# Seven products of quarters for three merged feed-forward weights, and one quad of tokens turned by VectorE

## The chip, the core and the metric

The kernel runs on one core of a Trainium2 chip. A core has several engines that each execute their own queue of instructions in order: TensorE (PE, matrix products; its weight loads are listed apart as PEld), VectorE (DVE), ScalarE (ACT), GpSimd (POOL) and SyncE (SP), which here only issues DMA transfers. They wait for each other by semaphores. Work lies in SBUF (128 partitions); PE writes into PSUM, of which the kernel uses two sides of four banks of 128x512 fp32 each. The metric is the device time of one execution in microseconds (us); lower is better. Everything is in fp32.

## The reference

The input x is 2 x 1024 tokens of 256. Four layers follow each other, each added to x:

```python
x = x + _L0_xattn_ref(_layernorm(x), ctx_1024, Wq, Wk, Wv, Wo, bo)    # attention in 4 windows, 8 heads of 64
x = x + _L0_ffn_ref(_layernorm(x), W1, b1, W2, b2)
x = x + _L1_xattn_ref(_layernorm(x), ctx_1024, ctx_1024, Wq, Wk, Wv, Wo)  # sigmoid scores, 16 heads of 16
x = x + _L1_ffn_ref(_layernorm(x), gamma_x, gamma_slot, slot_embeds, w1, w2)  # soft mixture of experts, 1024 slots

def _L0_ffn_ref(x, W1, b1, W2, b2):        # 8 groups of 256 tokens, each with weights of its own
    xg = x.reshape(8, 256, 256)
    h1 = jnp.einsum('gmh,goh->gmo', xg, W1) + b1[:, None, :]    # 1024 inner features
    h2 = jnp.einsum('gmo,gho->gmh', h1, W2) + b2[:, None, :]
    return h2.reshape(orig_shape)
```

The second layer has no non-linear step between its two products.

## The kernel before

**Tiling.** The 2048 tokens are four quads of 512 (`xq[0]` to `xq[3]`), each 4 tiles of 128 tokens. Quad q holds the tokens of the feed-forward groups 2q and 2q+1. The whole of x stays in SBUF.

**The feed-forward of layer 0.** Since it is linear, the two weights of a group g are first merged into one 256x256 matrix M_g = W1^T W2, with the bias row worked in. `product(g)` (L875) does it: 16 matmuls of 128x128 by 128x256 (L882; 8 chunks of the inner 1024 by 2 halves of the rows) sum into one PSUM bank `pmt`, a copy brings it to SBUF as `mt_g`, and POOL adds the bias b2 on one row (L891). Then `prepare(g+1)` subtracts, in place, the first column of the next group's W1 from the others (ACT at L865 and L869). The weights of a group lie in a tile `wg` (both factors and the first column apart), of which three exist, so that later groups load while earlier ones are used.

`norm_ff(q)` (L899) makes the normed tokens of a quad: `layernorm` (L824) calls `normed` (L814), which takes the moments on DVE, a power -1/2 on POOL and then subtracts and scales on DVE into `hn`; POOL sets the first column to 1; and `transposed` (L128) turns the 512 tokens with eight PE transposes into two PSUM banks `pt_f`, copied to `hT_f`. `feed_forward(q)` (L903) then takes, for both of the quad's groups, four matmuls with `hT_f` as the stationary operand and `mt_g` as the moving one, into `po`, and DVE adds `po` to x (L917).

**Turning tokens without PE.** Two other ways are in the kernel. `turned` (L149) lets DVE turn every 32x32 square in place of its tile, four instructions per quad (L137), into a tile `tr`; sixteen transfers of 32 KB, issued by SP (L158), then bring the squares to their places in the turned quad. `turned_by_square` (L163) takes the same four DVE instructions, then one transfer to DRAM (L170, `d_a`) and four back (L172). `turned` is used in layer 1's mixture of experts (`tr_m` to `xhT`), `turned_by_square` for the queries of layer 1 (`tr_a` to `hTa`) and the slots (`tr_se`). The tiles `hn`, `hT` and `tr` each come from the pool `lnp`, which has two buffers for each of these names: a third `tr` takes the buffer of the first and waits until the transfers out of that one have ended.

**The order of the work.** Around the change the source reads (L1120 to L1142, then L1266 to L1349): attention of layer 0 for quad after quad, between it the products 1 to 4, then `product(5)`, `feed_forward(1)`, `product(6)`, `norm_ff(2)`, `feed_forward(2)`, `slot_norms`, `norm_queries(0)`, `product(7)`, `norm_ff(3)`, `norm_queries(1)`, `norm_queries(2)`, the sums `pvs` (L1281), `queries(0)` (`pq`, L1240), and then the loop over quads of layer 1's attention. There, for q = 0: scores `psg` of the first half (L1308), their tanh on ACT (L1317), `feed_forward(3)`, the outputs `poT` (L1340), scores of the second half, `queries(1)`, and so on. This order is not the order of execution: a scheduler of the framework puts each engine's instructions into a queue at build time, by its own estimates of when each could run, and the engines then execute these queues strictly in order. Only a few instructions are pinned to the order of the source (`keep_in_program_order`, used with `late`), and the later stages have an order written by hand. So a change in one place can move other instructions in the queues, of DVE and of SP's transfers too. SP's queue issues the transfers of both turnings; a transfer that must wait for its data holds up those behind it.

**The names in the changed stretch** (60 to 120 us of the profile): `wg` weights, `pmt` and `mt` merged weights, `e` the softmax terms of layer 0's attention, `hn_f`, `pt_f`, `hT_f` the normed, turned tokens of the feed-forward, `po` its outputs, `tr_a`, `d_a`, `hTa` the queries' turned tokens, `pq` and `psg` the queries and scores of layer 1.

Of the kernel before, what the change touches and what calls it, by code (L numbers as in the profile page):

```python
# [9 lines left out]
FP = mybir.dt.float32  # L10
AF = mybir.ActivationFunctionType
ALU = mybir.AluOpType
# [3 lines left out]
P = 128  # L16
B = 2
S = 1024
D = 256
DC = D // P  # L20
NK = 64
QT = 4
# [12 lines left out]
OC = FF // P  # L35
# [10 lines left out]
SQ = 32  # L46
R4 = P // SQ
# [5 lines left out]
def tile_kernel(  # L53
# [19 lines left out]
    nc = tc.nc  # L73
# [9 lines left out]
    def bank(name, side=0):  # L83
        return ps[side].tile([P, 512], FP, tag="bank", name=name)
# [43 lines left out]
    def transposed(src, dst, name, side=0, out=nc.any.tensor_copy):  # L128

        for c in range(DC):  # L130
            pt = bank(f"pt_{name}_{c}", side)
            for t in range(QT):
                nc.tensor.transpose(pt[:, ts(t, P)], src[:, t, ts(c, P)], ident)
            out(dst[:, c, :], pt)
# [7 lines left out]
    def squares(src, tr, late=False):  # L142

        for t in range(QT):
            turn = square(src[:, t, 0:D], tr, t)
            if late:
                tc.keep_in_program_order(turn)

    def turned(src, dst, tr):  # L149

        squares(src, tr)
        to = dst.rearrange("p c (t i n) -> p (c t) i n", t=QT, i=R4)
        for i in range(R4):
            for r in range(R4):
                nc.sync.dma_start(  # L158
                    out=to[ts(r, SQ), :, i, :],
                    in_=tr[ts(i, SQ), r].rearrange("p c t n -> p (c t) n"),  # L160
                )
# [434 lines left out]
    def tt(dst, x, y, op):  # L596
        nc.vector.tensor_tensor(dst, x, y, op)  # L597
# [201 lines left out]
    with (  # L799
# [24 lines left out]
        def layernorm(xt, name, side=0, out=nc.any.tensor_copy):  # L824

            hn = normed(xt, name, 1)
            nc.gpsimd.memset(hn[:, :, 0:1], 1.0)
            hT = lnp.tile([P, DC, QN], FP, tag="hT", name=f"hT_{name}")
            transposed(hn, hT, name, side, out)
            return hT  # L830

# [2 lines left out]
        ffc = wide.enter_context(tc.tile_pool(name="ffc", bufs=1))  # L834
        weights = {}
# [20 lines left out]
        def prepare(g):  # L856
            if g not in weights:
                load_group(g)
            w1g, _, first = weights[g]
            less = ffc.tile([P, OC], FP, name=f"less_{g}")  # L860
            for part, scalar in enumerate((g > 0, g > 0)):
                ocs = range(part * OC // 2, (part + 1) * OC // 2)
                some = slice(ocs.start, ocs.stop)
                if scalar:
                    nc.scalar.activation(less[:, some], first[:, some, 0], AF.Copy, scale=-1.0)  # L865
                for oc in ocs:
                    w = w1g[:, oc, 1:]
                    if scalar:
                        last_prepared[g] = nc.scalar.activation(  # L869
                        w, w, AF.Identity, bias=less[:, oc : oc + 1]  # L870
                    )
                    else:
                        nc.vector.tensor_scalar(w, w, first[:, oc, :], None, ALU.subtract)  # L873

        def product(g):  # L875
            if g == 0:
                prepare(0)
            w1g, w2g, _ = weights[g]
            pm = bank(f"pmt_{g}", 1)
            for oc in range(OC):  # L880
                for hc in range(DC):
                    nc.tensor.matmul(  # L882
                        pm[:, ts(hc, D)],
                        lhsT=w1g[:, oc, ts(hc, P)],
                        rhs=w2g[:, oc, :],
                        start=(oc == 0 and hc == 0),
                        stop=(oc == OC - 1 and hc == DC - 1),
                    )
            mt = ffc.tile([P, DC, D], FP, name=f"mt_{g}")
            nc.any.tensor_copy(mt, pm.rearrange("p (c n) -> p c n", c=DC))  # L890
            nc.gpsimd.tensor_tensor(mt[0:1, 0, :], mt[0:1, 0, :], b2r[:, g, :], ALU.add)  # L891
            mts.append(mt)
            if g + 1 < NG:
                prepare(g + 1)


        hTfs = {}

        def norm_ff(q, side=0):  # L899
            out = nc.any.tensor_copy if q < QB else nc.scalar.copy  # L900
            hTfs[q] = layernorm(xq[q], f"f0_{q}", side, out)

        def feed_forward(q, side=0):  # L903
            for i in range(QN // GN):
                g = q * (QN // GN) + i
                xg = xq[q][:, ts(i, 2), :]
                po = bank(f"po_{g}", side)
                for t in range(2):
                    for dc in range(DC):
                        nc.tensor.matmul(  # L910
                            po[:, ts(t, D)],
                            lhsT=hTfs[q][:, dc, ds(i * GN + t * P, P)],
                            rhs=mts[g][:, dc, :],
                            start=(dc == 0),
                            stop=(dc == DC - 1),
                        )
                nc.vector.tensor_tensor(  # L917
                    xg, xg, po.rearrange("p (t d) -> p t d", t=2), ALU.add
                )
# [7 lines left out]
        with tc.tile_pool(name="p0", bufs=1) as p0, tc.tile_pool(name="a0", bufs=2) as a0:  # L927
# [25 lines left out]
            load_quad(3)  # L953

            product(0)


# [22 lines left out]
            for c in range(C0):  # L980
                for dc in range(DC):
                    nc.tensor.matmul(
                        pk[:, ts(c, P)],
                        lhsT=wk0s[:, dc, ts(c, P)],
                        rhs=hcT[:, dc].rearrange("p b j -> p (b j)"),
                        start=(dc == 0),
                        stop=(dc == DC - 1),
# [5 lines left out]
            for c in range(C0):  # L993
                for dc in range(DC):
                    nc.tensor.matmul(
                        pv[:, ts(c, P)],
                        lhsT=wv0s[:, dc, ts(c, P)],
                        rhs=hcT[:, dc].rearrange("p b j -> p (b j)"),
                        start=(dc == 0),
                        stop=(dc == DC - 1),  # L1000
# [9 lines left out]
            for dc in range(DC):  # L1010
                pws = [bank(f"pwk_{dc}_{e}") for e in range(2)]
                for c in range(C0):
                    for e in range(2):
# [3 lines left out]
                            lhsT=wq0s[r, c, ts(dc, P)],  # L1017
                            rhs=kT[r, c, :],
                            start=True,
                            stop=True,  # L1020
# [8 lines left out]
            for g in range(NBW // 2):  # L1029
                pw = bank(f"pvw_{g}")  # L1030
                for i in range(2):
                    for c in range(C0):
                        nc.tensor.matmul(
                            pw[ds(32 * c, 32), ts(i, D)],
                            lhsT=vblk[:, c, 2 * g + i].rearrange("p e j -> p (e j)"),
                            rhs=wo0s[:, c, :],
                            start=True,
                            stop=True,
# [61 lines left out]
            def attend(q):  # L1100
                if q not in atTs:
                    turn_weights(q)
                atT = atTs[q]
                for i in range(2):
                    po = bank(f"po0_{q}_{i}")
                    for k in range(2):
                        t = 2 * i + k
                        nc.tensor.matmul(  # L1108
                            po[:, ts(k, D)],
                            lhsT=atT[:, ts(t, P)],  # L1110
                            rhs=vw[:, (q * QT + t) // 2, :],
                            start=True,
                            stop=True,
                        )
                    xi = xq[q][:, ts(i, 2), :]
                    nc.vector.tensor_tensor(
                        xi, xi, po.rearrange("p (t d) -> p t d", t=2), ALU.add
                    )
# [16 lines left out]
            load_layer1()  # L1135
            norm_ff(1)
            attend(3)
        product(5)
        feed_forward(1)
        product(6)  # L1140
        norm_ff(2)
        feed_forward(2)  # L1142

        with (
            tc.tile_pool(name="a1c", bufs=1, side="right") as a1c,
# [35 lines left out]
            for c in range(C1):  # L1181
                for dc in range(DC):
                    nc.tensor.matmul(
                        pk[:, ts(c, P)],
                        lhsT=wk1s[:, dc, ts(c, P)],
                        rhs=ctxd[:, dc],
                        start=(dc == 0),
                        stop=(dc == DC - 1),
# [13 lines left out]
            for dc in range(DC):  # L1202
                nc.tensor.matmul(
                    pv[:, 0:D],
                    lhsT=ctxd[:, dc].rearrange("p b s -> p (b s)"),
                    rhs=wv1s[:, dc, :],
                    start=(dc == 0),
                    stop=(dc == DC - 1),
# [5 lines left out]
            for b in range(B):  # L1214
                for e in range(2):
                    to = vblk1[e * NK : (e + 1) * NK, b, :, e, :]
# [63 lines left out]
            for c in range(C1):  # L1280
                nc.tensor.matmul(  # L1281
                    pvs[:, ts(c, B)],
                    lhsT=vals[:, ts(c, NPR)].rearrange("p r e d -> p (r e d)"),
                    rhs=in_batch,
                    start=True,
                    stop=True,
# [7 lines left out]
            for q in range(NQ):  # L1294
                b = q * QN // S
                oTs[q] = a1.tile([P, C1, QN], FP, tag="oT", name=f"oT_{q}")
                for c in range(C1):
# [8 lines left out]
                    for j in range(NPR):  # L1306
# [3 lines left out]
                            lhsT=kblk[r, c, b].rearrange("p e s -> p (e s)"),  # L1310
                            rhs=qTs[q][r, c, :],
                            start=True,
                            stop=True,
# [25 lines left out]
                    for j in range(NPR):  # L1339
                        nc.tensor.matmul(  # L1340
                            po[ds(32 * j, 32), :],
                            lhsT=vblk1[:, b, NPR * c + j].rearrange("p e d -> p (e d)"),
                            rhs=sg[:, j, :],
                            start=True,
                            stop=True,
# [153 lines left out]
```

## Time and profile before

| | us |
|---|---|
| median of 3 runs | 423.4 (423.31 to 423.4) |
| profiled execution, device time | 423.25 |
| its span, first to last instruction | 421.5 |
| PE busy / DVE / ACT / POOL | 415.9 / 315.6 / 131.1 / 74.1 |
| product of one group on the chain (16 matmuls, L882) | 6.91 |
| all `pmt` matmuls (L882, 256 records) | 58.3 |
| eight transposes of quad 3's tokens on the chain (L133) | 0.87 |
| transfer of 32 KB by L158 (`xhT`), issue to landing, median | 2.0 |
| transfers back from DRAM by L172 (`hTa`), median | 3.1 |

The profile gives start and length of each instruction of one execution, with the engine and the line of the source, and for idle time the event that ended it. The device time contains 1.75 us that lie outside the span of the instructions. Busy shares say how full an engine is; the chain of waits, followed back from the last instruction, says which work set the end. Waiting on an engine that isn't on this chain costs nothing by itself. Durations of short DVE instructions overlap slightly: one takes 0.68 us from start to end at 128x512, and the next can start 0.60 us after it did; the distance from start to start is called the pitch here.

### The profile page before, as it was taken

The numbers are of one execution on the slowest core, as the hardware profiler recorded it, in microseconds if no ns is written. First come the engines' busy times: TensorE is split into PE (matmuls) and PEld (weight loads), VectorE is DVE, ScalarE is ACT, GpSimd is POOL, SyncE is SP. The second block draws the span as 40 slices with busy tenths as digits, with TensorE's granted clock in tenths as the row PEclk, the third lists the DMA queues.
The fourth block names the chain that finished last, engine by engine and source line by source line (L and its number), as shares of the span: only waits on it lengthen the run. The fifth ranks groups of instructions, "written<-read, shape, count | busy, mean of one in ns | idle before, by whom it ended". The sixth has DMA issues, their size and how long they took to land.

```text
span 421.5 us, 6298 instructions
## 1 busy us (share of the span) xinstructions
PE 415.9 (99%) x2270; PEld 310.3 (74%) x2270; DVE 315.6 (75%) x711; ACT 131.1 (31%) x266; POOL 74.1 (18%) x86
## 2 busy tenths in 40 slices
PE   8999999999999999999999999999999999999996
PEld 7889988888444454444488644899998864499996
DVE  2677777745578669978769889977985589776956
ACT  1145938513544522344641654300000004420000
POOL 2113233211101220104948900000000000000000
PEclk9999999999999999999999999999999999999999
DMA  6999983413633332120052764450022576520003
GB/s 256 416 415 425 402 340 134 168 47 112 149 102 105 46 47 31 29 43 2 0 213 101 129 97 74 65 89 2 0 84 49 121 120 98 89 44 2 2 2 100
DMA packets 99425, 50.03 MB, mean 119 GB/s; under 512 B 87873, under 2 KB 94401, under 8 KB 97857
## 3 DMA queue, kind: packets, MB, share of 16 engines
q1 hardware_dynamic: 99394, 49.63, 42.2%
q8 instruction: 18, 0.29, 0.3%
q14 instruction: 13, 0.11, 0.1%
HBM read 32.74 MB, written 6.30 MB: 93 GB/s over the span
## 4 chain that ended last, share of the span: by engine, by line
PE 86%; DVE 7%; SPq 2%; DMA 2%; issue 1%; POOL 1%; ACT 0%; DVEq 0%
PE psl L409 13%; PE pmt L882 13%; PE pc L586 12%; PE pp L586 12%; PE pmh L511 10%; PE pl L256 7%; PE pq L1240 3%; PE po L910 3%; SPq L158 2%; PE psc L1058 2%; PE pf L1254 2%; PE po L1108 2%; PE psg L1308 2%; PE poT L1340 1%; DMA wg<-in_wff_dram 1%
## 5 line engine op out<-in xcount | busy, mean ns | idle before, releaser
L882 PE MATMUL pmt<-wg 128*128 128x256 f32 x256 | 58.3, 384 | 0.3 <-DVE wg L873 0.3
L409 PE MATMUL psl<-xh,lg 128*128 128x258 f32 x256 | 56.8, 381 | 0.0
L256 PE MATMUL pl<-seT,xhT 128*128 128x512 f32 x128 | 56.1, 594 | 0.2 <-DVE rmax L275 0.2
L882 PEld LDWEIGHTS pmt<-wg 128*128 128x128 f32 x256 | 48.8, 193 | 7.5 <-DVE wg L873 0.7
L409 PEld LDWEIGHTS psl<-xh,lg 128*128 128x128 f32 x256 | 48.2, 190 | 7.4 <-issue 0.5
L256 PEld LDWEIGHTS pl<-seT,xhT 128*128 128x128 f32 x128 | 24.1, 190 | 29.2 <-issue 25.7
L395 POOL TENSOR_TENSOR lg<-lg,mb 128x1024 f32<-128x1024 f32 x13 | 33.2, 2594 | 26.9 <-ACT mb L203 25.3
L279 ACT ACTIVATE ec<-lg,nm 128x1024 f32<-128x1024 f32 x16 | 18.4, 1149 | 39.7 <-DVE nm L264 37.7
L586 PEld LDWEIGHTS pp<-ms,mh 128*128 128x128 f32 x256 | 29.4, 192 | 1.6 <-issue 1.0
L586 PE MATMUL pp<-ms,mh 128*128 128x128 f32 x256 | 30.2, 276 | 0.3
L521 ACT ACTIVATE mh<-mh 128x512 f32<-128x512 f32 x32 | 19.2, 627 | 21.1 <-DVE mh L557 19.6
L511 PE MATMUL pmh<-slT,ms 128*128 128x512 f32 x48 | 24.2, 592 | 0.0
L869 ACT ACTIVATE wg<-wg,less 128x255 f32<-128x255 f32 x56 | 23.4, 495 | 0.1
L1317 ACT ACTIVATE sg<-psg 128x512 f32<-128x512 f32 x32 | 16.5, 603 | 18.2 <-PE psg L1308 18.2
L586 PE MATMUL pp<-m_sums,mh 128*128 128x128 f32 x192 | 22.1, 275 | 0.0
L586 PE MATMUL pc<-pr,ec 128*128 128x128 f32 x192 | 22.1, 275 | 0.0
L586 PEld LDWEIGHTS pc<-pr,ec 128*128 128x128 f32 x192 | 21.8, 192 | 0.0
L586 PEld LDWEIGHTS pp<-m_sums,mh 128*128 128x128 f32 x192 | 21.8, 192 | 0.0
L398 ACT ACTIVATE lg<-lg 128x1024 f32<-128x1024 f32 x16 | 16.1, 1045 | 18.3 <-POOL lg L395 18.3
L545 ACT COPY mh<-pmh 128x512 f32<-128x512 f32 x8 | 4.6, 569 | 50.2 <-PE pmh L511 50.2
L308 DVE STREAM_TRANSPOSE tr<-ec 128x512 f32<-128x512 f32 x32 | 19.7, 674 | 0.0
L597 DVE TENSOR_TENSOR mh<-mh,mh 128x1024 f32<-128x1024 f32 x16 | 18.5, 1218 | 0.5 <-PE pp L586 0.5
(193 smaller groups left out, 669.8 us busy)
## 6 DMA issues: line engine op xcount, KB each, us to landing
wg<-in_wff_dram SPq DMA_DIRECT2D x5, 2052.0 KB, 10.1
ec<-tr SPq DMA_DIRECT2D x128, 64.0 KB, 2.3
wg<-in_wff_dram SPq DMA_DIRECT2D x4, 1026.0 KB, 12.9
xT<-in_xT_dram SPq DMA_DIRECT2D x4, 512.0 KB, 13.9
x<-in_x_dram SPq DMA_DIRECT2D x4, 512.0 KB, 16.1
d_a<-tr_a SPq DMA_DIRECT2D x4, 512.0 KB, 2.6
hTa<-d_a SPq DMA_DIRECT2D x16, 128.0 KB, 3.1
xhT<-tr_m SPq DMA_DIRECT2D x64, 32.0 KB, 2.0
```

The lines of the kernel that those rows point to most:

```text
L256: nc.tensor.matmul(pl, lhsT=xhTs[q][:, dc, ts(t, P)], rhs=in_order(seT[:, n], dc), start=(dc == 0), stop=(dc == DC - 1),)
L279: nc.scalar.activation(ecs[q][:, :, t, :], lg.rearrange("p (h n) -> p h n", h=2), AF.Exp, bias=nm[:, 1:2], scale=-1.0, accum_out=zcs[b][:, ...
L308: ins = nc.vector.transpose(tr[:, :, :, t, :].rearrange("p r c n -> p c r n"), half[:, t, :].rearrange("p (c r n) -> p c r n", c=EC // 2, ...
L395: engine.tensor_tensor(lgs[b][s], lgs[b][s], mbs[b], ALU.add)
L409: nc.tensor.matmul(pz[:, 0:XW], lhsT=lgs[b][s][:, ts(c, P)], rhs=xhs[b * QB + s // QT][:, s % QT, :], start=(s == 0), stop=(s == ST - 1),)
L511: nc.tensor.matmul(to, lhsT=lefts[i][:, ts(j, P)], rhs=in_order(slTs[b][0], i) if i < 2 else rights[b][i], start=True, stop=True,)
L521: nc.scalar.activation(h, h, AF.Gelu)
L586: nc.tensor.matmul(to, lhsT=left(k, m), rhs=right[:, k, :], start=(k == 0), stop=(k == QT - 1),)
L597: nc.vector.tensor_tensor(dst, x, y, op)
L869: last_prepared[g] = nc.scalar.activation(w, w, AF.Identity, bias=less[:, oc : oc + 1])
L882: nc.tensor.matmul(pm[:, ts(hc, D)], lhsT=w1g[:, oc, ts(hc, P)], rhs=w2g[:, oc, :], start=(oc == 0 and hc == 0), stop=(oc == OC - 1 and hc ...
L1317: nc.scalar.activation(sg[:, j, :], psgs[j], AF.Tanh, scale=0.5 * DH1**-0.5)
```

## The change

For groups 5, 6 and 7 (`FEWER`) the merged weight is made from quarters. Both factors are cut in two along the inner 1024 features (the sum) and in two along the 256 columns, and M_g, cut into four 128x128 blocks, is made from seven products of quarters instead of eight (Winograd's form of Strassen's method). `sum_quarters(g)` makes the sums and differences of quarters, eight DVE instructions of 128x512 each (two of them in place in the weights, six in a new tile `qs`), and is called right after `prepare(g)`. `product_of_quarters(g)` takes 7 x 4 matmuls of 128x128 by 128x128 into two PSUM banks; an ACT copy and seven DVE additions of 128x128, which read PSUM, make the four blocks of `mt_g`. The bias add on POOL stays. The tile `qs` of group 6 lies in a pool `qp` that is opened before `product(5)` and closed after `feed_forward(2)`, those of 5 and 7 share one in `ffc`.

For the last quad of the feed-forward (`f0_3`) `layernorm` calls `turned` in place of `transposed`: four DVE square transposes into a `tr` tile of `lnp` and sixteen transfers on SP instead of eight PE transposes and two copies.

```diff
@@ -826,6 +826,11 @@
             hn = normed(xt, name, 1)
             nc.gpsimd.memset(hn[:, :, 0:1], 1.0)
             hT = lnp.tile([P, DC, QN], FP, tag="hT", name=f"hT_{name}")
+            if name in ('f0_3',):
+
+                tr = lnp.tile([P, R4, DC, QT, SQ], FP, tag="tr", name=f"tr_{name}")
+                turned(hn, hT, tr)
+                return hT
             transposed(hn, hT, name, side, out)
             return hT
 
@@ -872,26 +877,88 @@
                     else:
                         nc.vector.tensor_scalar(w, w, first[:, oc, :], None, ALU.subtract)
 
+        FEWER = (5, 6, 7)
+        HO = OC // 2
+        quarter_sums, sums_in = {}, [ffc]
+
+        def quarters(w):
+
+            return [[w[:, ts(k, HO), ts(i, P)] for i in range(2)] for k in range(2)]
+
+        def sum_quarters(g):
+            w1g, w2g, _ = weights[g]
+            qs = sums_in[-1 if g == 6 else 0].tile([P, 6, HO, P], FP, tag="qs", name=f"qs_{g}")
+            s1, s2, s4, t1, t2, t4 = (qs[:, i] for i in range(6))
+            (b11, b12), (b21, b22) = quarters(w2g)
+            tt = nc.vector.tensor_tensor
+            tt(t1, b12, b11, ALU.subtract)
+            tt(t2, b22, t1, ALU.subtract)
+            tt(b12, b22, b12, ALU.subtract)
+            tt(t4, b21, t2, ALU.subtract)
+            (a11, a21), (a12, a22) = quarters(w1g)
+            tt(s1, a21, a22, ALU.add)
+            tt(s2, s1, a11, ALU.subtract)
+            tt(a21, a11, a21, ALU.subtract)
+            tt(s4, a12, s2, ALU.subtract)
+            quarter_sums[g] = [
+                (a11, b11), (a12, b21), (s2, t2), (a21, b12), (s1, t1), (s4, b22), (a22, t4)
+            ]
+
+        def product_of_quarters(g):
+
+            pms = [bank(f"pmt_{g}_{i}", 1) for i in range(2)]
+            p1, p2, p6, p7, p5, p3, p4 = (
+                pms[i // 4][:, ts(i % 4, P)] for i in range(7)
+            )
+            for to, (left, right) in zip((p1, p2, p6, p7, p5, p3, p4), quarter_sums[g]):
+                for k in range(HO):
+                    nc.tensor.matmul(
+                        to,
+                        lhsT=left[:, k, :],
+                        rhs=right[:, k, :],
+                        start=(k == 0),
+                        stop=(k == HO - 1),
+                    )
+            mt = ffc.tile([P, DC, D], FP, name=f"mt_{g}")
+            u = ffc.tile([P, 3, P], FP, tag="u", name=f"u_{g}")
+            (c11, c12), (c21, c22) = [[mt[:, c, ts(i, P)] for i in range(2)] for c in range(2)]
+            u1, u2, u3 = (u[:, i] for i in range(3))
+            tt = nc.vector.tensor_tensor
+            nc.scalar.copy(u1, p1)
+            tt(u2, p6, u1, ALU.add)
+            tt(c11, p2, u1, ALU.add)
+            tt(u3, p7, u2, ALU.add)
+            tt(c22, p5, u3, ALU.add)
+            tt(u2, p5, u2, ALU.add)
+            tt(c12, p3, u2, ALU.add)
+            tt(c21, p4, u3, ALU.add)
+            return mt
+
         def product(g):
             if g == 0:
                 prepare(0)
             w1g, w2g, _ = weights[g]
-            pm = bank(f"pmt_{g}", 1)
-            for oc in range(OC):
-                for hc in range(DC):
-                    nc.tensor.matmul(
-                        pm[:, ts(hc, D)],
-                        lhsT=w1g[:, oc, ts(hc, P)],
-                        rhs=w2g[:, oc, :],
-                        start=(oc == 0 and hc == 0),
-                        stop=(oc == OC - 1 and hc == DC - 1),
-                    )
-            mt = ffc.tile([P, DC, D], FP, name=f"mt_{g}")
-            nc.any.tensor_copy(mt, pm.rearrange("p (c n) -> p c n", c=DC))
+            if g in FEWER:
+                mt = product_of_quarters(g)
+            else:
+                pm = bank(f"pmt_{g}", 1)
+                for oc in range(OC):
+                    for hc in range(DC):
+                        nc.tensor.matmul(
+                            pm[:, ts(hc, D)],
+                            lhsT=w1g[:, oc, ts(hc, P)],
+                            rhs=w2g[:, oc, :],
+                            start=(oc == 0 and hc == 0),
+                            stop=(oc == OC - 1 and hc == DC - 1),
+                        )
+                mt = ffc.tile([P, DC, D], FP, name=f"mt_{g}")
+                nc.any.tensor_copy(mt, pm.rearrange("p (c n) -> p c n", c=DC))
             nc.gpsimd.tensor_tensor(mt[0:1, 0, :], mt[0:1, 0, :], b2r[:, g, :], ALU.add)
             mts.append(mt)
             if g + 1 < NG:
                 prepare(g + 1)
+                if g + 1 in FEWER:
+                    sum_quarters(g + 1)
 
 
         hTfs = {}
@@ -1135,11 +1202,14 @@
             load_layer1()
             norm_ff(1)
             attend(3)
+        qp = ExitStack()
+        sums_in.append(qp.enter_context(tc.tile_pool(name="qp", bufs=1)))
         product(5)
         feed_forward(1)
         product(6)
         norm_ff(2)
         feed_forward(2)
+        qp.close()
 
         with (
             tc.tile_pool(name="a1c", bufs=1, side="right") as a1c,
```

## The prediction

> **What bounds the kernel now.** I read the page first: the span, the busy shares and slices, and the shares of the chain of waits.
>
> ```profile
> span 421.5 us, 6298 instructions
> PE 415.9 (99%) x2270; PEld 310.3 (74%) x2270; DVE 315.6 (75%) x711; ACT 131.1 (31%) x266; POOL 74.1 (18%) x86
> PE   8999999999999999999999999999999999999996
> PE 86%; DVE 7%; SPq 2%; DMA 2%; issue 1%; POOL 1%; ACT 0%; DVEq 0%
> ```
>
> TensorE (PE) is busy 99% of the span, in every slice after the first; removed PE time is worth its length, if what replaces it keeps up. So I read the stretch of the change next, in windows of 10 us, to see how much room VectorE (DVE) has beside PE.
>
> ```profile
> core 0: us, PE busy (x) PEld busy (x) DVE busy (x) ACT busy (x) POOL busy (x), PEclk, DMA share, GB/s
> 70.00:80.00 10.00, 10.00 (x48) 8.57 (x47) 6.91 (x25) 6.72 (x22) 3.74 (x5) 1.00 0.61 243
> ...
> 90.00:100.00 10.00, 9.89 (x50) 8.79 (x50) 8.45 (x26) 2.53 (x9) 1.62 (x3) 1.00 0.22 65
> 100.00:110.00 10.00, 10.00 (x48) 6.52 (x47) 3.08 (x9) 4.61 (x9) 0.80 (x3) 1.00 0.57 177
> ```
>
> PE has no gap, at clock 1.00; DVE is already 69 to 84% busy up to 100 us. Third, the chain of waits in order of time (start, length, engine, tile, line) gives the path that is cut and lengthened, and the pitch of L158's transfers.
>
> ```profile
> 82.03 6.91 PE pmt L882 x32
> ...
> 95.37 6.91 PE pmt L882 x32
> 102.28 0.87 PE pt_f L133 x8
> ...
> 103.49 3.54 PE pq L1240 x8
> ...
> 108.11 3.65 PE po L910 x16
> ...
> 113.82 3.63 PE pq L1240 x8
> ...
> 146.74 0.61 SPq L158
> 147.35 0.04 issue
> 147.40 0.61 SPq L158
> ```
>
> Last the timeline of DVE and SP, and the landing times of L158's transfers (first of the two lines) and of those into hTa (second).
>
> ```profile
> 60.10 0.69 DVE L1070 TENSOR_TENSOR e<-psc,mx 128x512 f32<-128x512 f32 x1
> 78.09 1.38 DVE L818 TENSOR_SCALAR hn_f<-x,mv_f,rstd_f 128x255 f32<-128x255 f32 x4 [1.47 <-POOL rstd_f L125]
> 132.01 1.38 DVE L232 TENSOR_SCALAR xh<-x,mv_m,f 128x256 f32<-128x256 f32 x4
> 134.75 0.69 SPq L158 DMA_DIRECT2D xhT<-tr_m  x1
> DMA to landing us min/median/max: 1.9/2.0/3.4
> DMA to landing us min/median/max: 2.6/3.1/3.8
> ```
>
> Quad 3's normed tokens hn_f_3 exist at 79.5 us and are used at 108.11. That slack is what the change lives on.
>
> **What PE loses.** A product is 16 matmuls of 128x256 in 6.91 us, 0.432 each. Quarters need 7 x 4 = 28 of 128x128. The nearest row is psc (L1058): 8 such in 1.78 us on the chain, 0.223 each, so 6.24 us: 0.67 saved, 2.0 for three. That row pays 0.223, not half of 0.432, so an eighth of the arithmetic gives 10% of the time. The 8 transposes of hT_f_3 (0.87) go too. PE: -2.87 by 103.49.
>
> **What DVE gains.** Sums: 8 tensor_tensor of 128x512 per group, 24. Rows of that shape (L557 to L563) start 0.60 apart where independent, 0.72 where each needs the last; the quarters' own strided form stands at L597 with 684 ns, the same as plain ones. I take 0.60: 14.4 us; the other bound is 17.3. Outputs: 7 per group from PSUM, 128x128. No before row has exactly that form; from below, fixed cost plus length by the 512 and 1024 forms gives 0.29 busy, pitch 0.20; from above L750's 343 ns, pitch 0.26. I take 0.20. ACT gets one 128x128 copy per group and half of hT_f_1's copy, which the scheduler moves over from DVE, and loses three copies of 128x512 and two of hT: cover is ample (2.5 us busy of 10 at 90 to 100 us). The bias add on POOL now follows DVE instead of ACT; POOL is at 16% there.
>
> [...]
>
> **What moves.** DVE executes its queue in order. In the built order hn_f_3 now stands behind all 24 sums, the 14 outputs of products 5 and 6, the adds of quads 1 and 2 (L917) and the first query quad's four 32x32-square transposes (L137). Walking the queue from the end of e at 60.70: 24 x 0.60 = 14.4; 14 x 0.20 = 2.8; ten other 512-wide operations 6.0; eight hn rows x 0.325 = 2.6; four squares x 0.34 = 1.35; statistics 4.1; the rest 0.9; two waits on POOL's rstd 2.7 (1.47 each in the row above, part hidden). Sum 34.8: hn_f_3 starts at 95.5 instead of 78.09. A check on it: with the sums free, the L917 add of quad 2's last half (group 5) would still wait for PE to about 92.5 and not 93.3, so cheaper sums bring little.
>
> From hn to the first transfer the same sequence took 2.74 (132.01 to 134.75): first issue 98.25. Sixteen at a pitch of 0.65 (the chain's SPq rows plus issue): the last at 98.25 + 15 x 0.65 = 108.0; landing 2.0 (1.9 to 3.4): **110.0**. PE reaches the feed-forward of quad 3 at about 107.4: it began at 108.11, there is 2.87 less ahead of it, but the second set of scores now stands ahead (1.07) and must wait for the four tanh of the first set to free the banks: four times 603 ns by the page's row of L1317 against 1.07 for the matmuls, some 1.1 left over. So 108.11 - 2.87 + 1.07 + 1.1 = 107.4, and PE waits 2.6 there. Then po (3.65) and poT (1.0): 114.65.
>
> SP's queue is where the stall goes on. hTa_0's five transfers, and two of vblk1, go between and before the sixteen: its last piece is issued at 96.75 and lands 3.07 later, 99.8, against a need at 100.6 (103.49 - 2.87). 0.8 us of cover. But d_a_1, d_a_2 and the pieces of hTa_1 are now behind the sixteen. Moreover tr_a_2 shares a ring of two buffers with tr_f_3: DVE stands until the sixteen have landed (110.0), with tr_se_0, the adds of po_6 and po_7 and quad 3's statistics queued behind. Squares 1.42: 111.5; d_a_2's issue 0.44, which stands ahead of hTa_1's pieces; their first at 111.95, the last three pitches of 0.47 later at 113.35; landing 3.1 (2.6 to 3.8): **116.5**. queries(1), at 113.82 before, needs them; PE, ready at 114.65, waits 1.8 more. From there the two orders agree and PE is dense, so all moves by 116.5 - 113.82 = **+2.7**. In a sum: -2.87 (PE), +1.1 (scores placed early; their own 1.07 only changes place), +2.6 and +1.8 (two waits) = +2.6; with the rounding of the steps +2.7, which I keep.
>
> [...] The row: the longest gap after the start was 0.37 us, clock 1.00 throughout. [...]
>
> **Range.** DVE 3% cheaper or dearer: +2.0 or +4.2. Outputs at 0.26: +3.6. Sums 0.05 dearer each: +3.9. hTa landing 2.6 or 3.8: +2.2 or +3.4. The sixteen landing 0.6 later: +3.3. Small matmuls 5% dearer move little, as PE waits anyway; sums costing nothing still leave +2.3, and sixteen transfers costing SP nothing +2.1.
>
> **Rivals.**
> (1) The faster side: the last of the sixteen lands before PE comes. It needs landing by 106.7 and hTa_1 by 110.9; then 423.25 - 2.87 = 420.4. For it: hn_f_3 was ready at 79.5, and 26 us would be ample if the transfers were early. Against: the built DVE order puts 17 us ahead of it. Chance 0.05.
> (2) Only the first wait decides: hTa_1's pieces land by 114.65. Then +0.8 to +1.2, 424.1 to 424.5. For: with a landing of 2.6 and a DVE a little faster, half the second wait is gone. Against: tr_a_2's wait is on the same landing, and the chain behind it is 6.5 us long. Chance 0.13, of which 0.07 falls within 0.2%.
> (3) More than one wait: DVE dearer than its rows (dependent sums at 0.72, 2.9 us more, of which most arrives), or product 6 waits on its sums (1.8 us of cover) or hTa_0 (0.8): +4.2 to +5.6, 427.4 to 428.9. For: eight sums are partly chained. Against: rows at L557 to L563 are partly chained too. Chance 0.2.
> (4) The sums do not fit at all, DVE becomes the bound from product 5 on: over 429. Against: 34.8 us of DVE stand beside 35 of PE, with waits for POOL inside. Chance 0.04.
>
> **How the numbers follow.** Likeliest (0.58): +2.7 on the profiled run's 423.25 (span 421.5 and 1.75 around it); the median of the runs is 0.15 above it, so 426.1, its own range 425.2 to 427.2. Taking in most of (3) and the upper end of (2): 424.6 to 428.8. Outside lie (1), half of (2), (4): nearly 2 in 10. About 0.2%, 0.85 us, is what this measurement can tell from no change: faster is (1) with a little, 0.06; same is part of (2), 0.07; slower 0.87.
>
> **What would show it.** In the changed profile: products 5 to 7 at 6.2 to 6.3 us each; hn_f_3 at about 95.5; sixteen L158 issues from 98 to 108; the feed-forward of quad 3 waiting 2 to 3 us for a DMA into hT_f near 110; the third tr_a waiting for the same; queries(1) at about 116.5, waiting for DMA into hTa; a constant shift from there. Wrong if products stay at 6.9, if hn_f_3 starts before 90, if PE runs through 105 to 117 without gaps, or if the shift is taken back after 120.

## The result and the profile after

| | before | changed |
|---|---|---|
| median, us | 423.36 (422.93 to 423.4) | 429.45 (428.74 to 429.86) |
| ratio, 95% interval | | 1.0145 (1.0127 to 1.0162) |
| profiled execution | 423.25 | 428.74 |
| its span, and what lies outside it | 421.5, 1.75 | 426.6, 2.14 |

The change made the kernel 6.1 us slower by the medians and 5.5 us by the profiled executions. A second set of runs on another occasion gave 428.95 against 423.04, ratio 1.0133 (1.0117 to 1.0148).

From the page of the changed kernel, the busy shares, PE's and PEclk's slices, and the chain's shares:

```profile
span 426.6 us, 6504 instructions
PE 415.3 (97%) x2334; PEld 311.2 (73%) x2334; DVE 335.2 (79%) x759; ACT 129.8 (30%) x265; POOL 74.7 (18%) x86
PE   8999999999789999999999999999999999999996
PEclk9999999999899999999999999999999999999999
PE 66%; DVE 17%; SPq 7%; DMA 6%; issue 2%; POOL 1%; ACT 0%; DVEq 0%
```

PE's busy time hardly fell (415.9 to 415.3), and two slices near 110 us aren't full any more. The chain, 86% PE before, now runs 30% through DVE, SP's queue and DMA (11% before). Where it does so is seen in the chain in order of time (start, length, engine, tile, line):

```profile
91.35 0.35 DVE tr_a L137
...
96.26 1.38 DVE hn_f L818 x4
97.64 1.34 DVE tr_f L137 x4
99.05 0.69 SPq L158
99.78 0.62 SPq L158
...
108.28 0.61 SPq L158
108.93 1.94 DMA hT_f<-tr_f
111.00 1.44 DVE tr_a L137 x4
112.45 0.34 SPq L170
112.92 0.35 SPq L172
...
114.66 3.64 DMA hTa<-d_a
118.30 0.14 issue
118.43 3.67 PE pq L1310 x8
```

That is the path the prediction had drawn: hn_f_3 late on DVE, sixteen transfers on SP, tr_a_2 waiting for them to land, then d_a_2 and the pieces of hTa_1 to queries(1) (L1310 in this kernel). PE's own timeline has the two waits and one thing more:

```profile
98.40 1.06 PE L915 MATMUL pmt<-wg,qs 128*128 128x128 f32 x8
99.30 1.06 PE L915 MATMUL pmt<-qs,wg 128*128 128x128 f32 x8
100.19 0.51 PE L1351 MATMUL pvs<-in_batch,vals 128*128 128x2 f32 x4
100.55 3.68 PE L1310 MATMUL pq<-hTa,w1s 128*128 128x512 f32 x8
...
105.97 2.59 PE L1378 MATMUL psg<-qT,kblk 32*128 32x512 f32 x8 [0.67 <-ACT sg L1387]
111.01 5.11 PE L977 MATMUL po<-mt,hT_f 128*128 128x256 f32 x16 [2.45 <-DMA hT_f<-tr_f]
116.05 1.07 PE L1410 MATMUL poT<-sg,vblk 128*32 128x512 f32 x8
118.43 3.67 PE L1310 MATMUL pq<-hTa,w1s 128*128 128x512 f32 x8 [1.32 <-DMA hTa<-d_a]
```

queries(0) starts at 100.55. In the same view of the kernel before it starts at 103.35 (the chain's 103.49 counts from the end of the matmuls ahead of it, which overlap with it). So PE did lose 2.8 us of work. Then come 2.45 us of waiting for hT_f and 1.32 for hTa, and between them feed_forward(3) takes 5.11 instead of 3.7. The windows around it (PE, PEld, DVE, ACT, POOL busy, then the granted clock) say why:

```profile
105.00:110.00 5.00, 2.89 (x12) 1.17 (x8) 3.75 (x16) 4.03 (x8) 1.56 (x5) 1.00 0.36 54
110.00:115.00 5.00, 3.99 (x12) 3.35 (x13) 3.71 (x10) 0.00 (x0) 0.00 (x0) 0.66 0.66 226
115.00:120.00 5.00, 3.68 (x18) 1.66 (x17) 3.23 (x11) 0.00 (x0) 0.56 (x2) 1.00 1.04 241
```

PE was 58% busy from 105 to 110, and the clock granted from 110 to 115 was 0.66.

### The profile page after: what moved, and what is told of

Read it like the earlier page. It is cut to its first block, busy times and chain, and to the rows that moved or that the text cites. A ratio compares the mean times of both kernels' runs of the same rounds, so it can differ in the third digit from the quotient of the medians.

```text
span 426.6 us, 6504 instructions
## 1 busy us (share of the span) xinstructions
PE 415.3 (97%) x2334; PEld 311.2 (73%) x2334; DVE 335.2 (79%) x759; ACT 129.8 (30%) x265; POOL 74.7 (18%) x86
## 4 chain that ended last, share of the span: by engine, by line
PE 66%; DVE 17%; SPq 7%; DMA 6%; issue 2%; POOL 1%; ACT 0%; DVEq 0%
PE pc L586 12%; PE pp L586 11%; PE pmh L511 9%; PE pl L256 7%; PE psl L409 7%; PE pmt L947 6%; SPq L158 4%; PE pq L1310 3%; SPq L325 2%; PE psc L1125 2%; PE pf L1324 2%; DVE lg L264 1%; DMA wg<-in_wff_dram 1%; DMA max<-max 1%; PE poT L1410 1%
## 5 line engine op out<-in xcount | busy, mean ns | idle before, releaser
L947 PE MATMUL pmt<-wg 128*128 128x256 f32 x160 | 36.2, 381 | 1.1 <-DVE wg L878 1.1
L947 PEld LDWEIGHTS pmt<-wg 128*128 128x128 f32 x160 | 30.0, 191 | 5.7 <-DVE wg L878 1.7
L597 DVE TENSOR_TENSOR mh<-mh,mh 128x1024 f32<-128x1024 f32 x16 | 18.5, 1219 | 0.5 <-PE pp L586 0.5
```

Of the source, the lines that this page charges most:

```text
L947: nc.tensor.matmul(pm[:, ts(hc, D)], lhsT=w1g[:, oc, ts(hc, P)], rhs=w2g[:, oc, :], start=(oc == 0 and hc == 0), stop=(oc == OC - 1 and hc ...
```

## The experiments

Two questions were open: is it the queues (theory Q: hTa_1 comes late over VectorE and SyncE), the clock (theory C), or the price of one part (sums, turn); and which smaller change keeps the gain? Times are medians, with the ratio to the kernel before of the same occasion (423.04 to 423.17 us).

| run | us | ratio, 95% interval |
|---|---|---|
| e1 quarters only | 427.55 | 1.0102 (1.0089 to 1.0115) |
| e2 turn only | 421.83 | 0.9969 (0.9957 to 0.9981) |
| e3 groups 5 and 7, turn | 423.26 | 1.0008 (0.9996 to 1.0020) |
| e4 matmuls in the waits, first try | 429.46 | 1.0148 (1.0134 to 1.0163) |
| e5 the changed kernel again | 428.95 | 1.0133 (1.0117 to 1.0148) |
| e6 matmuls in the waits, late operands | 428.66 | 1.0128 (1.0114 to 1.0142) |
| e7 no sums | 421.22 | 0.9957 (0.9944 to 0.9969) |
| e8 groups 6 and 7, d_a_2 after hTa_1 | 421.66 | 0.9965 (0.9953 to 0.9978) |
| e9 groups 5 and 7, d_a_2 after hTa_1 | 422.39 | 0.9980 (0.9971 to 0.9989) |
| e10 group 5 only, turn | 423.79 | 1.0019 (1.0008 to 1.0030) |
| e11 own tile for tr_f_3 | 429.61 | 1.0154 (1.0140 to 1.0167) |
| e12 own tile and matmuls | 428.51 | 1.0125 (1.0109 to 1.0142) |

**e2, the turn alone.**

```diff
-        FEWER = (5, 6, 7)
+        FEWER = ()
```

> The changed kernel with no product from quarters (FEWER empty): quad 3's tokens are turned by VectorE and sixteen transfers, nothing else. Theory Q: hn_f_3 starts at 78 us as before, the sixteen transfers end long before TensorE needs them, no wait; the eight transposes are saved: 423.4 - 0.8 = 422.6 us. Theory T (sixteen transfers on SyncE delay the queries' tokens wherever they stand): 424 us or more, queries(1) waiting for hTa.

Measured 421.83 us: 1.3 us faster than before. Theory T falls. The sixteen transfers themselves do no harm, because hn_f_3 is there at 78.1 us, as before:

```profile
78.10 1.38 DVE L818 TENSOR_SCALAR hn_f<-x,mv_f,rstd_f 128x255 f32<-128x255 f32 x4 [1.48 <-POOL rstd_f L125]
```

**e7, the products of quarters without their sums.**

```diff
-            tt(t1, b12, b11, ALU.subtract)
...
-            tt(s4, a12, s2, ALU.subtract)
+            s1, s2, s4, t1, t2, t4 = a11, a21, a12, b11, b12, b21
```

All eight instructions of a group go (the cut shows the first and the last), and with them the tiles `qs` and the pool `qp`.

> The changed kernel without the 24 sums and differences of quarters: the seven products take the quarters of the weights as they are, so the merged weights of groups 5 to 7 aren't those of the reference. The 28 matmuls, the outputs and the turn with its sixteen transfers stay. Theory Q: with 14.4 us less in VectorE's queue hn_f_3 starts at about 78.5 us, neither feed_forward(3) nor queries(1) waits, and the time is 2.8 us below before: 420.3 us. Rival (the seven outputs from PSUM, or the sixteen transfers, hold up the rest): 423 us or more.

Measured 421.22 us, 7.7 us below the changed kernel beside it, though 28 matmuls, outputs and transfers are the same. So the loss comes from the 24 sums: from their time in VectorE's queue, or from the order that the scheduler makes with them. This run takes both away at once. SyncE's timeline shows how: the first eight of the sixteen leave 17 us earlier than at 99.05.

```profile
82.12 5.32 SPq L158 DMA_DIRECT2D hT_f<-tr_f  x8
```

That it is 421.2 and not 420.3 fits two waits of PE in this run: 0.5 us for hTa at queries(1) and 1.0 us for the weights of an early product, where before had 0.3.

**e1, the quarters alone.**

```diff
-            if name in ('f0_3',):
+            if name in ():
```

> The changed kernel with quad 3's tokens turned by TensorE again (eight transposes and two copies on ScalarE, no sixteen transfers), the three products still from quarters. Theory Q (the end is set by when hTa_1 reaches queries(1), late because hn_f_3 stands behind the sums on VectorE, then sixteen transfers on SyncE, then the tr ring): both waits of 2.45 and 1.32 us go, queries(0) starts at about 101.5 (103.49 - 2.0), queries(1) near 111.8 instead of 118.4; in the built order the adds of quarters still delay VectorE, and walking the queues with the rows' durations leaves one new wait of about 2.4 us before the second half of output(0), so 423.8 us in all, 5.6 below the changed kernel. Theory S (the sums on VectorE are the cost by themselves): stays above 427.

Measured 427.55 us: 3.8 above the walk. The new wait was at the place foreseen, 1 us longer than foreseen, and it cost twice:

```profile
121.75 6.32 PE L1324 MATMUL pf<-w1s,oT 128*128 128x256 f32 x14 [3.45 <-DVE oT L1417]
```

VectorE's oT stood behind hn_a_3 and tr_a_3 in the queue; PE waited 3.45 us, and the 14 matmul records behind the wait took 6.32 us. In the profile of e10 sixteen such take 3.65, so 14 take 3.2: the granted clock, 0.61 and 0.71 in the two windows of 5 us from 120 on, cost another 3.1 us. Here no other wait hid it. By the number alone this is what theory S had said (above 427): most of the loss is there without the sixteen transfers, and in the profile it sits at this one wait and the clock behind it.

**e4 and e6, is it the clock?** Both put overwritten matmuls into the waits.

```diff
                 po = bank(f"po_{g}", side)
+                if g == 6:
+                    for _ in range(11):
+                        nc.tensor.matmul(po[:, 0:P], lhsT=ident, rhs=ident, start=True, stop=True)
```

and the same ahead of `pq` for q = 1; in e6 they read `sg[:, 3, 0:P]` and `xq[3][:, 3, 0:P]`, tiles that are ready late.

> The changed kernel with eleven more 128x128 matmuls, whose results are overwritten, ahead of feed_forward(3) and eleven ahead of queries(1) on TensorE, so that it is busy where it waited and its clock stays at 1.00. Theory Q: the matmuls of feed_forward(3) take 3.65 us again instead of 5.1, but queries(1) still waits for hTa and starts at 118.4: the time stays within 0.5 us of the changed kernel, 428.5 to 429.5. Theory C (the halved clock is what the forecast lacked): the time falls by the 1.4 us that po took longer, to 427.5 to 428.

> The changed kernel itself once more, as the measure for the runs beside it: 428.7 to 429.9 us. Theory Q (queues): feed_forward(3) waits about 2.5 us for hT_f and queries(1) starts at about 118.4 us whatever the granted clock is, since hTa_1 comes over VectorE and SyncE. Theory C (clock): runs with a lower granted clock are longer by 1 us or more.

> The changed kernel with eleven more 128x128 matmuls into po_6 ahead of feed_forward(3) that read the last tanh tile, and eleven into pq ahead of queries(1) that read the last tile of quad 3 after its add; their results are overwritten. So TensorE has work inside both waits and not before them. Theory Q: po takes 3.65 us again, queries(1) still starts near 118.4, time within 0.5 us of the changed kernel run beside it. Theory C: granted clock 1.00 in every window, and the time falls by 1 us or more below the changed kernel.

e4 did not cover the wait: the scheduler put its matmuls ahead of the second scores, and feed_forward(3) still waited 2.5 us. It tells something all the same. Two of its runs had a mean granted clock of 1.000 and took 428.5 and 428.89, two had 0.996 and took 430.04 and 430.34: 1.5 us between the pairs. In its profiled execution (430.04) queries(1) did not wait for hTa at all; the 0.41 us that PE waited for hTa were those of queries(0). Four runs tie the time to the clock here, they don't show that nothing else differed. e6 did cover the wait, and in its profiled execution the clock was 1.00 in every window from 105 to 120:

```profile
111.78 3.69 PE L982 MATMUL po<-mt,hT_f 128*128 128x256 f32 x16 [0.50 <-DMA hT_f<-tr_f]
115.40 1.06 PE L1419 MATMUL poT<-sg,vblk 128*32 128x512 f32 x8
116.40 2.72 PE L1316 MATMUL pq<-x,ident 128*128 128x128 f32 x22
119.47 3.67 PE L1318 MATMUL pq<-hTa,w1s 128*128 128x512 f32 x8 [0.35 <-DMA hTa<-d_a]
```

feed_forward(3) takes 3.69 again, and the time is 428.66 against 428.95 of the changed kernel beside it: the same. With the clock whole, queries(1) still waits for hTa_1, so the clock alone is not the cause, as theory C had it. Half of theory Q's text falls too: queries(1) came at 119.5, not 118.4, since the last of the sixteen transfers took 2.64 us to land instead of 1.94 and hTa_1's last piece 3.89 instead of 3.64. What a whole clock would give with the earlier landings, e6 doesn't show.

**e11 and e12, the ring of two.**

```diff
-                tr = lnp.tile([P, R4, DC, QT, SQ], FP, tag="tr", name=f"tr_{name}")
+                tr = own[0].tile([P, R4, DC, QT, SQ], FP, tag="trf", name=f"tr_{name}")
```

where `own[0]` is a pool with one buffer, opened after `qp.close()`; e12 adds the matmuls of e6 (eleven and six).

> The changed kernel with tr_f_3 in a tile of its own, so that tr_a_2 no longer waits in the ring of two for the sixteen transfers to land. Theory Q (SyncE's queue with the sixteen ahead of d_a_1 is the longer way): hTa_1 comes only about 0.5 us sooner, 428.4 us. Rival R (the ring's wait is what holds queries(1)): the 1.3 us wait at queries(1) goes and its start falls to 117.1: 427.6 us or less.

> Both of the earlier steps at once on the changed kernel: tr_f_3 in a tile of its own, and overwritten matmuls ahead of feed_forward(3) (eleven, on the last tanh tile) and ahead of queries(1) (six). Alone, the own tile brought hTa_1 to 117.4 us, but feed_forward(3) ran at half clock until 117.6; alone, the matmuls kept the clock, but hTa_1 landed at 119.3. Theory of two floors (queries(1) starts when both hTa_1 and TensorE are there, and either is late enough by itself): queries(1) starts near 117.8 and the time falls to about 427.2 us, 1.4 below the run with the matmuls alone. Rival (something further down sets the end): 428.5 or more.

Measured 429.61 and 428.51 us. In e11 d_a_2 was issued 2.0 us sooner. hTa_1's first piece left only 0.4 us sooner (112.52 against 112.92): it reads what d_a_1 wrote, and d_a_1, issued at 109.66 behind the sixteen, landed 2.8 us later. Still hTa_1 was there in time, and queries(1) started at 118.63 nevertheless, because PE itself came late:

```profile
111.00 6.70 PE L979 MATMUL po<-mt,hT_f 128*128 128x256 f32 x16 [2.44 <-DMA hT_f<-tr_f]
117.64 1.06 PE L1413 MATMUL poT<-sg,vblk 128*32 128x512 f32 x8
118.63 3.70 PE L1313 MATMUL pq<-hTa,w1s 128*128 128x512 f32 x8
```

feed_forward(3) took 6.70 us where e6 has 3.69, at a granted clock of 0.53 from 110 to 115 and 0.79 from 115 to 120. Rival R falls: the ring is not what holds the time up by itself. e11's median lies above that of e5, but its spans do not (425.7 to 427.1 us against 426.2 to 427.6): 2.1 to 4.0 us of its four times lie outside the span. Read with e6, two floors lie close together at queries(1): hTa_1's landing (118.3 in the changed kernel) and PE after a halved clock (117.1 there, 118.6 here). e12 was to remove both and missed: its clock fell already between 105 and 110, although PE was as busy there as in e6 and paused no longer (first e12, then e6; the granted clock is the third number from the end):

```profile
105.00:110.00 5.00, 3.98 (x26) 2.70 (x19) 3.75 (x16) 2.57 (x6) 1.73 (x5) 0.89 0.32 56
```

```profile
105.00:110.00 5.00, 3.99 (x28) 2.80 (x24) 3.75 (x16) 2.56 (x5) 1.63 (x5) 1.00 0.37 57
```

The eleven matmuls took 3.95 instead of 2.72 us, and queries(1) came at 119.0, on PE's account. That both floors removed bring 1.4 us is therefore not shown.

**e3, e8 and e9, two groups, and one transfer's place.**

```diff
-        FEWER = (5, 6, 7)
+        FEWER = (5, 7)
```

is e3. e9 is e3 and e8 has (6, 7), both with

```diff
+            if name == "a_2":
+                order.enter_context(tc.issue_after(turned_last[0]))
             nc.sync.dma_start(out=by_row, in_=tr.rearrange("p r c t n -> p r (c t n)"))
```

where `turned_last[0]` is the last of hTa_1's four.

> The changed kernel with quarters for groups 5 and 7 only, the turn by VectorE and sixteen transfers kept: 8 sums and 7 outputs fewer on VectorE. Theory Q: hn_f_3 starts at about 80.6 us instead of 96.3, and both waits vanish; TensorE saves 0.67 x 2 + 0.87 = 2.2, of which 2.0 is left: 421.3 us. Theory S (each group's sums cost about as much as the whole loss divided by three, 2 us): 425 to 427 us.

> The changed kernel with quarters for groups 6 and 7 only, and on SyncE the transfer d_a_2 issued behind hTa_1's four instead of ahead of them. In the run with groups 5 and 7 queries(1) waited 1.8 us for hTa_1, whose transfers stood behind d_a_2, which waited for VectorE's tr_a_2. Theory Q with that wait gone: hTa_1 lands at 111.4, queries(1) starts at 111.7, 2.0 us below before: 421.1 us. If VectorE's load itself is the cost: 423 us as with groups 5 and 7.

> The run with quarters for groups 5 and 7 and the turn by sixteen transfers (423.26 us), with one change: on SyncE d_a_2 is issued behind hTa_1's four transfers. Theory Q (d_a_2, waiting for VectorE's tr_a_2, held up hTa_1): hTa_1 lands near 110.5 instead of 114.0, queries(1) starts at 111.7 without its 1.8 us wait, and the time falls to about 421.5 us. If VectorE's load as such is what groups 5 and 7 cost: it stays at 423.

e3 gave 423.26: not the loss of theory S, but nothing of the gain either. SyncE's timeline in e3, and then in e9:

```profile
103.67 4.71 SPq L170 DMA_DIRECT2D d_a<-tr_a  x2
108.50 4.46 SPq L172 DMA_DIRECT2D hTa<-d_a  x8
```

```profile
103.47 0.55 SPq L175 DMA_DIRECT2D d_a<-tr_a  x1
106.36 1.73 SPq L177 DMA_DIRECT2D hTa<-d_a  x4
108.20 0.36 SPq L175 DMA_DIRECT2D d_a<-tr_a  x1
```

In e3 d_a_1 and d_a_2 are issued one behind the other, the second only once tr_a_2 is done at 108, and hTa_1 stands behind it until 108.5: queries(1) waits 1.8 us. In e9 hTa_1 leaves at 106.4, as soon as d_a_1 has landed, and that wait is gone. It gave 0.9 us instead of 1.8. In e9's profiled execution PE waits in later stages instead (1.0 us for xhT and 0.5 for VectorE), but that execution, 423.14, was the slowest of its eleven; where the rest of the gain went in the others is not shown. e8 is 421.66, 1.4 us faster than before; it can't be told from the turn alone (421.83).

**e10, one group.**

```diff
-        FEWER = (5, 6, 7)
+        FEWER = (5,)
```

> Quarters for group 5 alone (8 sums, 7 outputs), the turn by sixteen transfers kept. Theory Q: hTa_1 lands about 2.9 us before TensorE needs it, so nothing new waits; TensorE saves 0.67 + 0.87 = 1.5, and some 0.4 more further down as in the run with the turn alone: 421.2 us. If each group's quarters cost more on VectorE than they save on TensorE: above the turn alone, 422 to 423.

Measured 423.79, 2.6 above what was expected, although the stretch did as it should: queries(1) started at 112.73, 1.1 us earlier than before. In the profiled execution (424.01) the loss is far behind the change. First the line of VectorE's timeline and then that of GpSimd, for e10:

```profile
242.10 2.34 DVE L500 TENSOR_TENSOR sl_sums<-slT,sl_sums 128x512 f32<-128x512 f32 x1
```

```profile
228.81 15.08 POOL L395 TENSOR_TENSOR lg<-lg,mb 128x1024 f32<-128x1024 f32 x5 [4.59 <-DMA mb<-mrow]
```

and the same two for the kernel before:

```profile
242.64 0.69 DVE L500 TENSOR_TENSOR sl_sums<-slT,sl_sums 128x512 f32<-128x512 f32 x1
```

```profile
227.06 14.60 POOL L395 TENSOR_TENSOR lg<-lg,mb 128x1024 f32<-128x1024 f32 x5 [1.67 <-DMA mb<-mrow]
```

The small transfer mrow landed after 3.6 us instead of 1.4 in e10, so GpSimd's adds began and ended about 2 us later (until 243.9 instead of 241.7), and the VectorE add at 242.1, which now ran beside them, took 2.34 us instead of 0.69. PE's matmuls pmh waited 1.7 us for it, most of the 2.1 us by which this span (422.2) is longer than that of the turn alone (420.1). Why mrow landed late is not known.

## Why the prediction was wrong

The direction, the place and both waits were as predicted, the first wait's size by luck; the size of the whole was not: +2.7 stated, +5.5 (profiled) and +6.1 (medians) measured. Point by point:

- **PE's gain**: 2.87 predicted, 2.80 by queries(0). A quarter product was to take 6.24; in the rows of the changed kernel four matmuls (eight records) follow each other every 0.89 (99.30 to 100.19), 0.223 each, as taken from psc.
- **VectorE's walk**: hn_f_3 at 95.5 predicted, 96.26 measured. Its 24 sums took 14.97 us (14.4), one of them 1.15 alone; the 14 outputs 2.76 (2.8). That the outputs read PSUM cost nothing extra; in the kernel before, too, a 128x512 add takes 680 ns at L917, which reads PSUM, and 684 at L597 within SBUF.
- **First wait**: 2.6 predicted, 2.45 measured, and that is luck. The landing came at 110.87 instead of 110.0, and PE at 108.56 instead of 107.4, as the second scores with their wait for the tanh took 3.3 us where the sum had 1.07 + 1.1. The two errors cancel.
- **Second wait and the sum**: the step that failed is "landing 3.1 (2.6 to 3.8): **116.5**" with "so all moves by 116.5 - 113.82 = **+2.7**". queries(1) came at 118.43, +4.6. Of the 1.9 us missing, 0.97 had gathered by hTa_1's first piece (112.92 against 111.95: 0.76 from VectorE, 0.11 up to the last landing of the sixteen, the rest behind it); the three pitches of its pieces took 1.74 instead of 1.41; the landing took 3.64 instead of 3.1, and the issue 0.13. All four erred to the same side. The mis-sized terms of the sum are thus the landing, the pitches and the walk. The 3.1 was a median over four quads; in e9, where d_a_2 isn't issued just ahead of them, the pieces of hTa_1 landed after 2.9 to 3.0 us. The kernel before had shown the difference: there a transfer of the same 512 KB, d_se, stands just ahead of hTa_1's pieces, and these landed after 3.5 to 3.8 us and took SyncE 2.21 us, against 1.73 to 2.04 for the other quads (the lines are below the list).
- **"From there the two orders agree and PE is dense"**: in order, yes, but another 0.5 us came in later stages (the span grew by 5.1): PE waited 0.5 us for VectorE at 236 where it had not before, after the last of the transfers into max, from 219 on, had taken 5.4 us to land instead of 4.1. The prediction had no term for that.
- **Outside the span** 2.14 instead of 1.75: 0.4 us, without a term. The medians add 0.6 more, since the profiled execution was the shortest of the four. 4.6 + 0.5 + 0.4 + 0.6 = 6.1.
- **The clock**: the sum has no term for it and takes the matmuls as they ran at 1.00. In the first wait, 2.45 us behind a 0.67 us wait and small matmuls, it was halved (0.50 from 110.5 on): 5.11 us for feed_forward(3) instead of 3.65, and up to 6.70 in e11. In the profiled run this lay under the wait for hTa_1, and e6 shows the same time without it; but in e1 it cost 3.1 us in the open. That the term was missing did not show in this run, because the wait for hTa_1 covered it.
- **The range**: "sums costing nothing still leave +2.3" freed the sums inside the built order, a case that no run made. Built without them (e7) the order itself changes, hn_f_3 goes to its old place, and the kernel is 1.8 us faster than before. Taken together, the +2.3 and e7 say that the order made because of the sums costs more than their time; a run that keeps one of the two and drops the other is missing, so this stays argued.
- **Small readings**: the longest gap on PE before was 0.40 us (at 242.35), not 0.37; four times 603 ns less 1.07 is 1.3, not 1.1; and 3% of 34.8 us is 1.0, so DVE 3% dearer gives +3.7 by the sum, not +4.2. None of this changes the account.

The two lines of SyncE in the kernel before on which the remark on hTa_1's pieces rests:

```profile
106.64 0.34 SPq L170 DMA_DIRECT2D d_se<-tr_se  x1
107.07 2.21 SPq L172 DMA_DIRECT2D hTa<-d_a  x4
```

## What to carry to other kernels

In a kernel whose PE is full, adding work to an engine that is 70 to 80% busy was priced here by what the scheduler queued behind it, to the last transfer: rebuild without the added work and compare the orders, rather than set its durations to zero. A margin of 1 us over a chain of seven steps on three engines was none, as here the steps' errors all went to one side; a transfer is best priced by its own row, with what is issued ahead of it, and not by a median over its kind; and a wait on PE should be priced with the clock that may follow it (in the changed kernel a wait of 2.45 us, and about 3.4 us at 0.50). Of a change with two parts each is worth running alone: here the turn alone (421.83) is faster than before and the whole is slower, and with two groups and d_a_2 behind hTa_1 (421.66) some of the quarters can stay, without a gain over the turn alone that could be measured.

## What was not expected of the hardware

- **The clock after a short wait.** The granted clock halved within 2.45 us without a matmul (108.56 to 111.01), with PE 58% busy over the 5 us before 110. Read in steps of half a microsecond in the changed kernel, it stood at 1.00 up to 110.0, at 0.97 in the next step, at 0.50 from 110.5 to 113.5, at 0.61 up to 114.0 and at 1.00 again: about 3.4 us at half. For the other profiled executions the same is an estimate from the windows of 5 us, if the clock was either 1.00 or 0.50: about 3.4 us in e12 (0.89 and 0.77), and about 6.8 us in e1 (0.61 and 0.71), e5 (0.97, 0.50 and 0.85) and e11 (0.53 and 0.79). So feed_forward(3) took 5.11 us in the changed kernel and 6.36 in e5, behind gaps of 2.45 and 2.47 us; e11's gap was 2.44 and e1's 3.45. Such a gap isn't needed: in e12 the clock fell at about 108.9 (by the same estimate), after pauses of 0.67 and 0.35 us, when PE had been at work again since 107.60; e6, with the same pauses, kept 1.00. What lowers the clock, and for how long, no run here took apart.
- **VectorE beside GpSimd.** A 128x512 add from SBUF to SBUF took 2.34 us while GpSimd ran adds of 128x1024, and 0.69 after they had ended (e10 and before). What held the add up is not seen in the trace.
- **Time outside the span.** Executions of the kernel before (6298 instructions), of e1 to e3 and of e7 to e10 had 1.7 to 2.1 us outside the span; those of the changed kernel (6504 instructions), e4, e5, e6, e11 and e12 2.1 to 4.0. Its cause was not looked into.
